# Moving a chunk's reciprocal and its product with it from the end of one beat into the middle of the next

## The chip, the cores and the metric

The kernel runs on one core of one Trainium2 chip. The metric is the device time of one execution in microseconds (us). Before the change it is 4211.53 us, the median of three runs (4208.49 to 4213.91 us). All lines of a profile in this document come from one profiled execution, whose own time is told below.

The core has five engines that run side by side and wait for each other through semaphores. In the profile PE is the matrix engine and PEld its weight loads, DVE is the vector engine, ACT the engine of pointwise functions, POOL the general engine, and SP the queue from which this kernel issues all of its DMAs. Each of them works through its own list of instructions in order.

## The reference

Two layers over 8 batches of 2048 nodes with 256 features. Layer 0 is an attention whose softmax runs over *chunks* of 256 keys, each by itself; the results of the 8 chunks are added. Layer 1 is a graph attention over the whole row. Each layer is followed by a residual and a layer norm.

```python
# layer 0 (4 heads of 64), per batch
scores = jnp.einsum('bhnd,bhjcd->bhnjc', q, kc) / jnp.sqrt(Dh)
scores = jnp.clip(scores, -10.0, 10.0)
scores = jnp.where(mask == 0, -10.0, scores)
attn = jax.nn.softmax(scores, axis=-1)              # over c, the 256 keys of chunk j
ctx = jnp.einsum('bhnjc,bhjcd->bhnd', attn, vc)     # summed over the 8 chunks
out = layernorm(ctx.reshape(B, N, 256) @ Wo.T + bo + x) * gamma + beta
x = layernorm(x + out)
# layer 1
Wh = x @ W
e = leaky_relu(s_i[:, :, None] + s_j[:, None, :], 0.2)   # s = Wh @ a1, Wh @ a2
e = where(adj > 0 or diagonal, e, -inf)
x = layernorm(x + elu(softmax(e) @ Wh))
```

## The kernel before

**Tiles and beats.** The queries of a batch are cut into 4 blocks of 512. A block takes the 8 chunks of keys in turn, so there are 8 x 4 x 8 = 256 chunks, and a chunk takes two *beats*: an even one (`half` 0) and an odd one (`half` 1). A beat treats one tile of 128 keys for all four heads, as two score tiles of 128 x 1024. While chunk J gets its scores, the chunk before it (`prev`) gets its products with the values. Layer 1 of the batch before runs beside layer 0 in the same beats; batch 0 has no layer 1 beside it, and after the 512 beats of layer 0 the last batch's layer 1 runs alone.

**What a beat does, in the order in which it is written down.** Each engine gets its instructions in this order (the schedule is written by hand).

1. `begin_beat`: the exponentials of layer 1's weights that were made ready a beat ago (ACT, L765), then `leaky` of the next layer 1 steps (DVE, L754), one or two a beat: `RATE` is 1.5 steps a beat, and none where layer 1 has nothing ready.
2. The score matmuls of this beat (PE, L873), their *clips* against the mask (DVE, L884: it reads a tile in PSUM and a mask in SBUF), and the exponentials (ACT, L888). Where layer 1 has no steps open (`spare`), one score tile more is done ahead, with a third PSUM buffer.
3. `middle_of_beat`: `edges`, the second DVE operation of each layer 1 step (L760).
4. The products of `prev` (PE, L942). In the even beat these are part 2, the softmax denominators (with `ones` as weights), and part 0; in the odd beat part 1. ACT copies parts 0 and 1 to `un` (L950) and the denominators to `ds` (L956), and SP issues a DMA that lays them out as 128 x 16, `dc<-ds` (L958).
5. `end_beat`: layer 1's products (PE, L776); then the *generators*: `ahead` (`prelude` of the next layer 1 batch, with its `half_max` on DVE, L451, and its loads) and `fins` (`fin`, `fin1`, projections: output projections, statistics, norms); then the *agenda* of this beat.

**The reciprocal's path.** Three functions stand on the agenda. `inverse` is the DVE reciprocal of `dc` (L964) and a DMA of it to DRAM, `rd<-dc` (L966). `spread` is the DMA that broadcasts it to 128 partitions, `r<-rd` (L970, 256 KB); SP issues it when `rd` has landed. `scaled` is the DVE product `un<-un,r` (L977; L975 for a block's first chunk) and POOL's addition `ctxT<-ctxT,un` (L978). Outside batch 0 (`early` false) `inverse` and `spread` are at the end of the even beat E in which the denominators were made, and `scaled` is at the end of E+2. In batch 0 they are at the end of E+1 and of E+4. So DVE meets, at the end of each even beat, first the product of the chunk before and then the reciprocal of this chunk, and next `leaky` and the clips of the odd beat. The chunk's `un`, `dc`, `ds` and `r` have two buffers each.

**What waits for ctxT.** After a block's last chunk `scaled` notes its beat in `ctx_done`; `fin` does its output projection (PE, L370) in the next beat.

**Loads.** Masks of layer 0 are loaded at the start of an odd beat (one chunk in four), those of layer 1 in `begin_beat`, both by L140; `xT_q`, the input of the next block's query projection (`make_qT`, PE at L266), at the end of an odd beat, one chunk before it is used.

Of the kernel before, what the change touches and what calls it, by code (L numbers as in the profile page):

```python
# [28 lines left out]
def tile_adj_attention__then__gat(  # L29
# [88 lines left out]
    def xT_tile(b, ib, name):  # L118
        t = four.tile([P, KC, IB], F32, tag="xT", name=f"xT_{name}{b}_{ib}")
        nc.sync.dma_start(out=t, in_=xT[b, :, ts(ib, IB)].rearrange("(k p) n -> p k n", p=P))  # L120
        return t
# [16 lines left out]
    def mask_block(n, ib, hf, name):  # L138
        t = two.tile([P, HT, IB], I8, tag=f"mask{n}", name=f"mk{n}_{name}")
        nc.sync.dma_start(out=t, in_=mask[n][ib, hf])  # L140
        return t
# [209 lines left out]
    ctx_done = {}  # L351
# [370 lines left out]
    total = B * NIB * NCH  # L722
# [72 lines left out]
    l1_live = True  # L795
    ahead = [prelude(b) for b in range(B - 1)] + [last_prelude(B - 1)]
    edged, weighted = [], []
    agenda = {}
    beat = 0
    credit = 0.0  # L800
    RATE, LAST_RATE = 1.5, 1.3
# [1 line left out]
    def l1_open():  # L803
        return edged or weighted

    def at(when, fn):
        agenda.setdefault(when, []).append(fn)

    def begin_beat(rate):
        nonlocal l1_live, credit, edged, weighted, leaking  # L810
        weighted, edged = edged, []
        for s in weighted:
            s.weights()
        leaking = []
        credit = min(credit + rate, 2.0)
        while l1_live and credit >= 1.0:
            s = next(l1, False)
            if s is False:
                l1_live = False
            elif s is None:  # L820
                break
            else:
                credit -= 1.0
                leaking.append(s)
                s.leaky()

    def middle_of_beat():
        nonlocal edged
        for s in leaking:
            s.edges()  # L830
        edged = leaking
# [30 lines left out]
    prev = None  # L862
# [19 lines left out]
    def clip(sc, b, ib, n):  # L882
        cap = blocks0[b, ib, n // HT][:, n % HT, :].unsqueeze(1).to_broadcast([P, 2, IB])
        nc.vector.scalar_tensor_tensor(sc, sc, -CLIP, cap, ALU.max, ALU.min)  # L884

    def exponentials(chunk, n, hp, sc):
        e = eight.tile([P, 2, IB], F32, tag="e", name=f"e{b}_{ib}_{n}_{hp}")
        nc.scalar.activation(e, sc, AF.Exp)  # L888
        chunk["es"].append(e)

    for J in range(total + 1):
        b, ib, j = J // (NIB * NCH), J // NCH % NIB, J % NCH
        live = J < total
        if live and j == 0:
            ctxT = one.tile([P, 2, IB], F32, tag="ctx", name=f"ctxT{b}_{ib}")
        cur = {"b": b, "ib": ib, "j": j, "es": [], "ctxT": ctxT, "v": vs[min(b, B - 1)], "name": f"{b}_{ib}_{j}"}
        for half in range(2):
            c = 2 * j + half
            if live:

                if c % HT == 1:
                    n = (b * NIB + ib) * 2 + c // HT + 1
                    nb, nib, nhf = n // (2 * NIB), n // 2 % NIB, n % 2
                    if 0 < nb < B:
                        blocks0[nb, nib, nhf] = mask_block(0, nib, nhf, f"{nb}_{nib}_{nhf}")
            if ahead_sc is not None:
                exponentials(cur, c, 0, ahead_sc)
            begin_beat(RATE if b < B - 1 else LAST_RATE)
            if live:


                spare = not (l1_open() or leaking)
                todo = [(b, ib, c, hp) for hp in range(0 if ahead_sc is None else 1, NPAIR)]
                if spare and (b, ib, c + 1) != (0, 0, HT):
                    if c + 1 < NT:
                        todo.append((b, ib, c + 1, 0))
                    elif b == 0:
                        todo.append((*nxt, 0, 0))
                scs = [scores(*which) for which in todo]
                for which, sc in zip(todo, scs):  # L920
                    clip(sc, *which[:3])
                ahead_sc = None
                for which, sc in zip(todo, scs):
                    if which[2] == c:
                        exponentials(cur, c, which[3], sc)
                    else:
                        ahead_sc = sc
            middle_of_beat()

            early = J < NIB * NCH  # L930
            if prev is not None:
                if half == 0:

                    pool, tag = (one, "hr") if early and J % 3 == 2 else (two, "un")
                    prev["un"] = pool.tile([P, 2, IB], F32, tag=tag, name=f"un{prev['name']}")
                for part in ((2, 0), (1,))[half]:
                    m = ps_m.tile([P, IB], F32, tag="m", name=f"u{prev['name']}_{part}")
                    for i in range(2):
                        pc = 2 * prev["j"] + i
                        for h in range(H):  # L940
                            f0 = h * D + part * DH
                            nc.tensor.matmul(  # L942
                                m[h * DH : (h + 1) * DH, :],
                                prev["v"][pc // TPB][:, pc % TPB, f0 : f0 + DH] if part < 2 else ones[:, 0:DH],
                                prev["es"][2 * i + h // 2][:, h % 2, :],
                                start=(i == 0),
                                stop=(i == 1),
                            )
                    if part < 2:
                        nc.scalar.copy(prev["un"][:, part, :], m)  # L950
                    else:

                        ds = two.tile([P, IB], F32, tag="ds", name=f"ds{prev['name']}")
                        nc.scalar.copy(ds, m)  # L956
                        dc = two.tile([P, IB // DH], F32, tag="dc", name=f"dc{prev['name']}")
                        nc.sync.dma_start(  # L958
                            out=dc, in_=ds.rearrange("(h m) (n w) -> h m n w", m=DH, n=DH)[:, 0, :, :]
                        )  # L960
                        prev["dc"] = dc

                        def inverse(p=prev):
                            nc.vector.reciprocal(p["dc"], p["dc"])  # L964
                            p["rd"] = dram3.tile([H, IB], F32, tag="rd", name=f"rd{p['name']}")
                            nc.sync.dma_start(out=p["rd"].rearrange("h (m w) -> (h m) w", m=DH), in_=p["dc"])  # L966

                        def spread(p=prev):
                            p["r"] = two.tile([P, IB], F32, tag="r", name=f"r{p['name']}")
                            nc.sync.dma_start(out=p["r"], in_=p["rd"].unsqueeze(1).to_broadcast([H, DH, IB]))  # L970

                        def scaled(p=prev):
                            r2 = p["r"].unsqueeze(1).to_broadcast([P, 2, IB])
                            if p["j"] == 0:
                                nc.vector.tensor_mul(p["ctxT"], p["un"], r2)  # L975
                            else:
                                nc.vector.tensor_mul(p["un"], p["un"], r2)  # L977
                                nc.gpsimd.tensor_add(p["ctxT"], p["ctxT"], p["un"])  # L978
                            if p["j"] == NCH - 1:
                                ctx_done[p["b"], p["ib"]] = beat  # L980
                            if p["j"] == NCH - (5 if p["b"] == 0 else 4):
                                fins.append(fin(p["b"], p["ib"], p["ctxT"]))

                        lag = 1 if early else 0
                        at(beat + lag, inverse)
                        at(beat + lag, spread)
                        at(beat + 2 + 2 * lag, scaled)

            end_beat()
            if half == 1:  # L990

                sooner = 1 if b == 0 else 0
                if live and j == NCH - 2 - sooner and (b, ib) != (B - 1, NIB - 1):
                    nxt = (b, ib + 1) if ib + 1 < NIB else (b + 1, 0)
                    xq = xT_tile(*nxt, "q")
                if live and j == NCH - 1 - sooner and (b, ib) != (B - 1, NIB - 1):
                    make_qT(*nxt, xq)
            beat += 1
        prev = cur if live else None
# [51 lines left out]
```

## Time and profile before

| | |
|---|---|
| median of three runs | 4211.53 us |
| the profiled execution's own time | 4214.11 us |
| its span, first to last instruction | 4212.3 us |
| PE busy | 3930.2 us (93%) |
| DVE busy | 3234.6 us (77%) |
| ACT busy | 2183.5 us (52%) |
| POOL busy | 1112.8 us (26%) |
| mean granted TensorE clock | 0.981 |

The profiled execution is 2.6 us longer than the median of the runs. The span holds seven stretches of about 512 us, one for each batch of layer 0 (batch 0 up to about 510 us, then one batch with the layer 1 of the batch before beside it), an eighth that ends near 3985 us, and a tail of layer 1 alone. In the page of a profile, a row of a group gives how many instructions it had, its busy time, the mean length of one in ns, and after the bar the idle time of the engine just before them and what ended it. In a row of the timeline the first two numbers are start and length in us, and a bracket holds the idle time of the engine before it and who ended it.

### The profile page before, as it was taken

How to read it: one execution, taken by the hardware profiler on the slowest of the kernel's cores; microseconds unless marked ns; L12 is line 12 of the kernel's file. 1: busy time of each engine (PE TensorE's matmuls, PEld its weight loads, DVE VectorE, ACT ScalarE, POOL GpSimd, SP SyncE). 2: the span in 40 equal slices, each digit the busy share in tenths (PEclk: the TensorE clock that was granted, in tenths of full speed). 3: DMA queues.
4: the chain of work that ended last, by engine and by line, in shares of the span. 5: the costliest groups of instructions: out<-in, count | busy, mean ns of one | idle time of the engine just before them, and what ended most of it. 6: DMA issues, size and time to landing. Idle time of an engine off the chain costs nothing.

```text
span 4212.3 us, 67836 instructions
## 1 busy us (share of the span) xinstructions
PE 3930.2 (93%) x26677; PEld 1349.5 (32%) x26677; DVE 3234.6 (77%) x5038; ACT 2183.5 (52%) x3153; POOL 1112.8 (26%) x481
## 2 busy tenths in 40 slices
PE   9899899998999989999899998999989999899867
PEld 3223233332233322333233332323323333233222
DVE  5886698756987579875789757887588875887886
ACT  5665455555555545554555554455545555455434
POOL 0232322223223222222323222232222222232300
PEclk9999999999999999999999999999999999999989
DMA  5554332223322243221432214322142322432321
GB/s 175 183 169 149 102 108 86 67 67 108 104 82 67 61 126 101 77 64 52 132 98 81 67 51 133 91 81 68 57 134 84 90 65 66 124 94 72 123 87 56
DMA packets 282192, 400.00 MB, mean 95 GB/s; under 512 B 101872, under 2 KB 152944, under 8 KB 280975
## 3 DMA queue, kind: packets, MB, share of 16 engines
q1 hardware_dynamic: 281870, 395.66, 30.7%
q8 instruction: 209, 3.42, 0.3%
q14 instruction: 113, 0.92, 0.1%
HBM read 340.79 MB, written 52.69 MB: 93 GB/s over the span
## 4 chain that ended last, share of the span: by engine, by line
PE 63%; DVE 18%; DMA 7%; ACT 5%; issue 4%; POOL 1%; SPq 1%; DVEq 0%; ACTq 0%; POOLq 0%
PE u L942 20%; PE sc L873 15%; PE us L776 15%; DVE sc L884 6%; PE pk L266 3%; PE pv L285 3%; PE pq L266 3%; PE po L370 3%; DVE w L754 3%; PE pw L605 3%; DMA dc<-ds 2%; DVE w L760 2%; DVE fb L451 2%; DMA rd<-dc 2%; ACT e L888 1%
## 5 line engine op out<-in xcount | busy, mean ns | idle before, releaser
L888 ACT ACTIVATE e<-sc 128x1024 f32<-128x1024 f32 x1024 | 1040.2, 1023 | 1225.7 <-DVE sc L884 1196.3
L884 DVE SCALAR_TENSOR_TENSOR sc<-sc,mk 128x1024 f32<-128x1024 f32 x1024 | 1206.6, 1223 | 568.1 <-PE sc L873 487.2
L873 PE MATMUL sc<-qT,kT 64*128 64x512 f32 x4096 | 1045.5, 625 | 100.1 <-ACT e L888 99.9
L776 PE MATMUL us<-w,hb 128*32 128x512 f32 x8192 | 955.8, 601 | 76.5 <-ACT w L765 68.3
L978 POOL TENSOR_TENSOR ctxT<-ctxT,un 128x1024 f32<-128x1024 f32 x224 | 556.7, 2485 | 1715.8 <-DVE un L977 1552.5
L942 PE MATMUL u<-e,v 128*32 128x512 f32 x8192 | 979.1, 595 | 0.0
L873 PEld LDWEIGHTS sc<-qT,kT 64*128 64x128 f32 x4096 | 348.8, 187 | 727.0 <-issue 354.3
L754 DVE SCALAR_TENSOR_TENSOR w<-ab,sj 128x512 f32<-128x512 f32 x512 | 502.7, 1001 | 8.8 <-DMA ab<-ab_d 5.4
L942 PE MATMUL u<-e,ones 128*32 128x512 f32 x4096 | 505.3, 612 | 0.0
L776 PEld LDWEIGHTS us<-w,hb 128*32 128x32 f32 x8192 | 262.8, 111 | 712.0 <-issue 545.9
L942 PEld LDWEIGHTS u<-e,v 128*32 128x32 f32 x8192 | 240.3, 110 | 658.0 <-issue 520.8
L760 DVE SCALAR_TENSOR_TENSOR w<-w,sj,mk 128x512 f32<-128x512 f32 x512 | 393.4, 790 | 3.4 <-DMA mk<-mask 0.9
L950 ACT COPY un<-u 128x512 f32<-128x512 f32 x512 | 300.1, 586 | 152.5 <-PE u L942 143.9
L765 ACT ACTIVATE w<-w 128x512 f32<-128x512 f32 x512 | 306.4, 628 | 69.6 <-DVE w L760 60.7
L451 DVE CUSTOM_DVE_ANT_0 fb<-sj_row,fb 128x1024 bf16<-128x1024 f32 x240 | 336.4, 1412 | 5.0 <-DMA fb<-far 4.9
L977 DVE TENSOR_TENSOR un<-un,r 128x1024 f32<-128x1024 f32 x224 | 278.5, 1244 | 54.0 <-DMA r<-rd 53.8
L942 PEld LDWEIGHTS u<-e,ones 128*32 128x32 f32 x4096 | 108.5, 111 | 363.2 <-issue 301.5
L626 POOL TENSOR_TENSOR hx<-hx,hr 128x1024 f32<-128x1024 f32 x28 | 88.5, 3160 | 370.1 <-DVE hx L625 370.1
L964 DVE RECIPROCAL dc<-dc 128x16 f32<-128x16 f32 x256 | 63.6, 248 | 143.8 <-DMA dc<-ds 137.0
L956 ACT COPY ds<-u 128x512 f32<-128x512 f32 x256 | 148.7, 581 | 29.7 <-PE u L942 21.7
L266 PE MATMUL pq<-xT_q,WT_q 128*128 128x512 f32 x248 | 122.2, 634 | 39.6 <-DMA xT_q<-in_xT_dram 24.1
L266 PE MATMUL pk<-xT_k,WT_k 128*128 128x512 f32 x256 | 122.3, 621 | 18.0 <-ACT ds L956 10.2
(108 smaller groups left out, 2434.7 us busy)
## 6 DMA issues: line engine op xcount, KB each, us to landing
r<-rd SPq DMA_DIRECT2D x256, 256.0 KB
mk<-mask SPq DMA_DIRECT2D x120, 512.0 KB
fb<-far SPq DMA_DIRECT2D x240, 256.0 KB
xT_k<-in_xT_dram SPq DMA_DIRECT2D x32, 512.0 KB
raw<-in_adjT_dram SPq DMA_DIRECT2D x32, 512.0 KB
rawf<-in_adj_dram SPq DMA_DIRECT2D x32, 512.0 KB
x<-in_x_dram SPq DMA_DIRECT2D x32, 512.0 KB
h_d<-y SPq DMA_DIRECT2D x32, 512.0 KB
```

What stands on the lines that cost most here:

```text
L266: nc.tensor.matmul(pm, WT[name][:, k, ts(o, P)], xt[:, k, :], start=(k == 0), stop=(k == KC - 1))
L451: nc.vector.tensor_tensor_reduce(out=fb, in0=row, in1=fb, scale=1.0, scalar=2 * FAR * 0.999, op0=ALU.add, op1=ALU.max, accum_out=dst,)
L754: nc.vector.scalar_tensor_tensor(self.w, k["ab"][:, 0, :], k["sj"][:, 1, c : c + 1], k["ab"][:, 1, :], ALU.max, ALU.add)
L760: nc.vector.scalar_tensor_tensor(self.w, self.w, k["sj"][:, 0, c : c + 1], k["mks"][c // HT][:, c % HT, :], ALU.add, ALU.min)
L765: nc.scalar.activation(self.w, self.w, AF.Exp)
L776: nc.tensor.matmul(k["us"][g * DH : (g + 1) * DH, n, :], k["hb"][c // TPB][:, c % TPB, f0 : f0 + DH], self.w, start=first, stop=last,)
L873: nc.tensor.matmul(sc[:, h, :], kTs[b][n // TPB][h * D : (h + 1) * D, hp, ts(n % TPB, P)], qTs[b, ib][h * D : (h + 1) * D, hp, :], start=True,
L884: nc.vector.scalar_tensor_tensor(sc, sc, -CLIP, cap, ALU.max, ALU.min)
L888: nc.scalar.activation(e, sc, AF.Exp)
L942: nc.tensor.matmul(m[h * DH : (h + 1) * DH, :], prev["v"][pc // TPB][:, pc % TPB, f0 : f0 + DH] if part < 2 else ones[:, 0:DH], prev["es"] ...
L950: nc.scalar.copy(prev["un"][:, part, :], m)
L978: nc.gpsimd.tensor_add(p["ctxT"], p["ctxT"], p["un"])
```

## The change

`inverse` and `spread` of a chunk outside batch 0 leave the agenda of the even beat E. They go to a new list, `behind_clips`, and are written down in beat E+1 at the start of `middle_of_beat`: behind the clips and ahead of `edges`. `scaled` of every chunk leaves the agenda of its beat (its `due`) and goes to another new list, `behind_leaky`, of beat `due`+1: behind that beat's `leaky` and ahead of its clips. Only the last two chunks, whose `due` lies behind the last beat of layer 0, keep the agenda for `scaled`. `ctx_done` now holds `due` and not the beat in which `scaled` is written, so `fin` comes in the same beat as before.

On DVE an odd beat changes from [product, reciprocal at the end of the even beat], leaky, clips, edges to leaky, product, clips, reciprocal, edges. In batch 0, which has no leaky, the product keeps its place before the clips, and the reciprocal its own. On PE, ACT and POOL the order of the instructions is the same in both kernels. On SP `rd<-dc` and `r<-rd` move behind the mask loads of beat E+1, and stay ahead of the loads that the generators issue at its end.

```diff
-    agenda = {}
+    agenda, behind_leaky, behind_clips = {}, {}, {}
...
                 s.leaky()
+        for fn in behind_leaky.pop(beat, []):
+            fn()

     def middle_of_beat():
         nonlocal edged
+        for fn in behind_clips.pop(beat, []):
+            fn()
         for s in leaking:
             s.edges()
...
                             if p["j"] == NCH - 1:
-                                ctx_done[p["b"], p["ib"]] = beat
+                                ctx_done[p["b"], p["ib"]] = p["due"]
...
                         lag = 1 if early else 0
-                        at(beat + lag, inverse)
-                        at(beat + lag, spread)
-                        at(beat + 2 + 2 * lag, scaled)
+                        if early:
+                            at(beat + lag, inverse)
+                            at(beat + lag, spread)
+                        else:
+                            behind_clips[beat + 1] = [inverse, spread]
+                        prev["due"] = beat + 2 + 2 * lag
+                        if prev["due"] < 2 * total:
+                            behind_leaky.setdefault(prev["due"] + 1, []).append(scaled)
+                        else:
+                            at(prev["due"], scaled)
```

## The prediction

> **What bounds the kernel now.** I read the page first, then PE's own waits stage by stage, then the timeline around each of PE's gaps.
>
> ```profile
> span 4212.3 us, 67836 instructions
> PE 3930.2 (93%) x26677; PEld 1349.5 (32%) x26677; DVE 3234.6 (77%) x5038; ACT 2183.5 (52%) x3153; POOL 1112.8 (26%) x481
> L754 DVE SCALAR_TENSOR_TENSOR w<-ab,sj 128x512 f32<-128x512 f32 x512 | 502.7, 1001 | 8.8 <-DMA ab<-ab_d 5.4
> L977 DVE TENSOR_TENSOR un<-un,r 128x1024 f32<-128x1024 f32 x224 | 278.5, 1244 | 54.0 <-DMA r<-rd 53.8
> L964 DVE RECIPROCAL dc<-dc 128x16 f32<-128x16 f32 x256 | 63.6, 248 | 143.8 <-DMA dc<-ds 137.0
> ```
>
> The last row is what the change goes for: DVE stands 137 us before the reciprocal, waiting for `dc`. But DVE is not the bound. PE is busy 93% of the span, and only its 282 us of idle time can be won or added to. PE's waits in one batch's stretch (1536 to 2048 us):
>
> ```profile
> PE sc L873 <- ACT e L888: 13.6, 7, 6.1
> PE us L776 <- ACT w L765: 4.1, 3, 2.6
> PE pq L266 <- ACT un L950: 2.5, 2, 1.5
> PE po L370 <- POOL ctxT L978: 1.1, 1, 1.1
> PE us L776 <- ACT agg L791: 1.1, 1, 1.1
> PE pq L266 <- DMA xT_q<-in_xT_dram: 1.0, 1, 1.0
> PE pk L266 <- ACT ds L956: 1.0, 1, 1.0
> ```
>
> That is 24.4 us of 512, and the same list comes back in each of batches 1 to 6. So the question is which of these few gaps hang on an odd beat's clips. Only one of over a microsecond does in the open part of a batch (layer 1 beside), this one:
>
> ```profile
> 1794.47 1.22 DVE L977 TENSOR_TENSOR un<-un,r 128x1024 f32<-128x1024 f32 x1
> 1795.84 2.38 POOL L978 TENSOR_TENSOR ctxT<-ctxT,un 128x1024 f32<-128x1024 f32 x1 [5.39 <-DVE un L977]
> 1795.94 0.25 DVE L964 RECIPROCAL dc<-dc 128x16 f32<-128x16 f32 x1 [0.25 <-DMA dc<-ds]
> 1796.12 2.64 DVE L754 SCALAR_TENSOR_TENSOR w<-ab,sj 128x512 f32<-128x512 f32 x1
> 1798.68 2.35 DVE L884 SCALAR_TENSOR_TENSOR sc<-sc,mk 128x1024 f32<-128x1024 f32 x2
> 1799.93 2.16 ACT L888 ACTIVATE e<-sc 128x1024 f32<-128x1024 f32 x2 [2.22 <-DVE sc L884]
> 1801.98 0.58 ACT L950 COPY un<-u 128x512 f32<-128x512 f32 x1
> 1802.62 3.70 PE L266 MATMUL pq<-xT_q,WT_q 128*128 128x512 f32 x8 [1.53 <-ACT un L950]
> ```
>
> The leaky (L754) takes 2.64 us here and 0.66 us elsewhere (1602.21): it runs beside POOL's addition and ends 0.5 us behind it. Two clips beside such an addition keep their 2.3 us (1534.16 below; POOL adds from 1534.23). The largest gap lies at a batch's boundary, where layer 1 has run dry:
>
> ```profile
> 1526.52 0.54 SPq L970 DMA_DIRECT2D r<-rd  x1
> 1532.86 1.23 DVE L977 TENSOR_TENSOR un<-un,r 128x1024 f32<-128x1024 f32 x1 [6.74 <-DMA r<-rd]
> 1534.00 0.25 DVE L964 RECIPROCAL dc<-dc 128x16 f32<-128x16 f32 x1
> 1534.16 2.33 DVE L884 SCALAR_TENSOR_TENSOR sc<-sc,mk 128x1024 f32<-128x1024 f32 x2
> 1536.48 2.08 PE L873 MATMUL sc<-qT,kT 64*128 64x512 f32 x4 [6.12 <-ACT e L888]
> ```
>
> Here DVE waits for the broadcast itself, behind a burst of the prelude's loads.
>
> **The change, part by part.** No instruction is added or removed; DVE's reciprocal and product change places in the odd beat, and SP's `rd<-dc` and `r<-rd` come about one pair of clips later.
>
> *Reciprocal and product in the open part.* The reciprocal's wait goes (its cover is the leaky, the product and two clips, 4.2 us, where `dc` lands about 2 us after its issue), and POOL's addition then runs beside the clips and not beside the leaky. At 1794.47 the row becomes leaky 0.6, product 1.2, clips from 1796.3 and not 1798.68: 2.4 us earlier. The copy of `un` ends at about 1800.4, before PE ends the work ahead of `pq` at 1801.08, so the 1.53 us go. Batches 1 to 6 each have this gap: 6 x 1.53 = -9.2 us. A smaller gap of the same kind (0.31 us before the scores at 1634.80; leaky 2.62) goes too: -1.8 us. Ends: 0, if ACT is late for another reason, and -12. Everywhere else in the open part PE has no gap, and DVE's savings buy nothing there.
>
> *The last batch.* Three gaps have the same chain: 0.68 (3689.31), 1.21 (3811.89) and 2.38 us (3841.92; there DVE stands 3.23 us before the reciprocal). The clips come 2.4, 2.4 and 3.1 us earlier: -4.3 us. Ends: -1 and -5.
>
> *What does not move.* The gaps at 1582.73, 1714.01 and 1996.75 lie behind an even beat's clips, after statistics; those at 1586.84, 1720.73 and 2002.55 behind four or eight normalizations on ACT. The change touches neither. Batch 0 keeps its order.
>
> *The broadcast, later.* This is the cost. From the reciprocal it takes 0.3 us to issue `rd`, 1.4 to the issue of `r`, and 5.0 to 5.7 until a product that waits for it can start (1492.59 to 1497.57; 1509.84 to 1515.56): 6.7 to 7.4 us. Before, the product came 12 to 20 us after the reciprocal in the open part. There the reciprocal moves back by 3 to 5 us, the product by a leaky's 0.7 to 1.4; `r` still comes in time, by about a microsecond in the tightest chunk (1813.38 to 1825.51). At the boundary chunks are short: three reciprocals have their product 7.9, 7.4 and 7.7 us behind (1498.71, 1508.14, 1560.09). Moved behind the clips they have some 5.5 us, and the product, now in front of the clips, waits. The first two lie ahead of the 6.12 us gap; their slip (1 and 2.4 us) ends in it, because it ends when the prelude's burst lets `r` through, which does not move. That gap changes by the reciprocal's 0.16 us at 1534.00. The third has nothing behind it that absorbs: clips end 1562.74, reciprocal, `rd` 1563.0, `r` 1564.4, product at 1569.4 and not 1567.77; the clips, which waited for the reciprocal till 1569.85, start at 1570.55, and POOL's addition ends at 1573.1, where `po` started at 1572.38: +0.7 us a boundary (0 if `r` needs 4.3; +1.4 with 5.7).
>
> *The loads behind it.* On SP `r` of 1535.70 is now issued at about 1538.05, straight ahead of the loads that end with `xT_q`. PE waits for that load (1.04 us at 1547.97), then for ACT's copy (0.96 at 1550.88), which hangs on clips that DVE held for 3.40 us before a reciprocal. The second gap goes; the first grows by what the burst is late: the first load is issued 1 us later, and up to 1.5 us of `r`'s traffic falls into the burst. Net +0.4, ends -1.0 and +1.5. Together a boundary costs -0.1 + 0.7 + 0.4 = +1.0 us, seven times: +7.0; ends -7 and +20.
>
> [...]
>
> *The tail.* The last reciprocal but one (3963.15) goes behind clips that end at 3966.24; `r` is then there at about 3973, its product 2 us later than at 3970.81. DVE waits for the next reciprocal until 3973.58 today, so it loses little, but POOL's three additions (3972.46 to 3980.9, contended by DVE) shift: +1 us, ends 0 and +2.
>
> Sum: -9.2 - 1.8 - 4.3 + 7.0 + 1.0 = -7.3 us on the profiled execution's 4214.1 us (2.6 above the median): 4206.8 there, 4204.2 against the median of 4211.5, or 0.17% faster. A measurement of this kernel can tell about 0.2% (8.4 us) from no change.
>
> **Rivals.** *The broadcast's delay decides, slower.* In a boundary the product, its clips, the next reciprocal and the broadcast now form a loop: 1.2 + 2.3 + 0.2 + 6.7 = 10.4 us, where the short chunks turn in about 9.3. If the slip is not absorbed by the 6.12 us gap (it is if that gap still ends near 1536.5), a boundary pays 1.1 + 1.3 + 1.1 and 0.4 for the load: 3.9 us, times seven 27; with the gains of 15.3 and the tail, +13 us: 4224. It decides against the change from 2.0 us a boundary, and by 0.2% from 3.2.
> *A free boundary, clearly faster.* `xT_q` is no later and `r` needs 4.3 us: -1.0 a boundary, -22 us in all with the tail at +0.5: 4189. For it: the 0.96 us gap goes whatever the load does. Against it: the DMA engines are filled by that burst.
> *Nothing.* ACT or PE hold the odd-beat gaps, and the boundary pays nothing: 4211. For it: PE is full in the open part. Against it: the chain of 1802.62 is unbroken back to the leaky.
>
> **How the numbers follow.** Forecast 0.47, which lies around the bound (0.20 faster, 0.27 same); free boundary 0.20, faster; nothing 0.09, same; broadcast 0.24, of it 0.22 slower and 0.02 same. Faster 0.40, same 0.38, slower 0.22. The forecast's own range is 4197 to 4211; with the rivals' middle parts 4189 to 4224.
>
> **What the trace after would show.** Right: DVE's idle time before the reciprocal near 20 us, leaky's mean near 800 ns, no PE gap before the `pq` like 1802.62's; DVE's wait for `r` above 54 us, with waits of 1 to 3 us in each boundary; the gap like 1536.48's still 6 us; `pq` waiting 2 to 3 us for `xT_q`. Wrong: that gap at 8 us or more, new PE gaps before scores in the open part (then `r` is late there too), or a mid-batch `pq` that still waits for `un`. The prediction fails most easily on a transfer: all seven boundaries repeat one pattern, so 1 us misjudged there is 7 us.

## The result and the profile after

The changed kernel takes 4229.58 us, the median of five runs (4225.94 to 4235.57), beside 4210.15 for the kernel before on the same chip (five runs, 4204.95 to 4213.91). The ratio is 1.0047, with a 95% interval of 1.0036 to 1.0059: half a percent slower, where the forecast was 0.17% faster. The profiled execution took 4225.94 us, 11.8 more than that of before. The page of the changed kernel; the last three rows are groups by line, with the number of instructions, busy time, mean and the idle time in front:

```profile
span 4224.2 us, 67772 instructions
PE 3941.1 (93%) x26677; PEld 1350.2 (32%) x26677; DVE 3193.3 (76%) x5038; ACT 2183.0 (52%) x3153; POOL 1072.2 (25%) x481
L754 DVE SCALAR_TENSOR_TENSOR w<-ab,sj 128x512 f32<-128x512 f32 x512 | 442.4, 884 | 13.8 <-ACT w L765 8.3
L981 DVE TENSOR_TENSOR un<-un,r 128x1024 f32<-128x1024 f32 x224 | 304.2, 1358 | 103.8 <-DMA r<-rd 101.6
L968 DVE RECIPROCAL dc<-dc 128x16 f32<-128x16 f32 x256 | 62.2, 243 | 42.2 <-DMA dc<-ds 42.0
```

DVE's wait in front of the reciprocal fell from 137 to 42 us and a leaky's mean from 1001 to 884 ns, as the change meant. In return DVE stands 101.6 us before the product, waiting for the broadcast, and not 53.8. And PE is busy 10.9 us longer with the same 26,677 matmuls, while its idle time stayed what it was: 4224.2 - 3941.1 = 283 us, before 282. The waits of the changed kernel (total, times, longest):

```profile
DVE un L981 <- DMA r<-rd: 101.6, 40, 6.8
PE sc L877 <- ACT e L892: 101.1, 48, 6.8
DVE dc L968 <- DMA dc<-ds: 42.0, 18, 3.9
PE pq L266 <- DMA xT_q<-in_xT_dram: 41.8, 10, 6.6
PE po L370 <- POOL ctxT L982: 15.0, 15, 2.1
```

PE's wait for `xT_q` grew from 24.1 to 41.8 us; its wait for the copy of `un` ahead of `pq` (15.4 us, 12 times) is no longer in the list. The gap in mid-batch is gone as the prediction had it: leaky, product and clips follow each other, POOL's addition lies beside the clips, and `pq` starts without a wait (timeline of the changed kernel: start, duration, engine, line, idle time in brackets).

```profile
1802.02 0.75 DVE L754 SCALAR_TENSOR_TENSOR w<-ab,sj 128x512 f32<-128x512 f32 x1
1802.68 1.22 DVE L981 TENSOR_TENSOR un<-un,r 128x1024 f32<-128x1024 f32 x1
1803.81 2.36 DVE L888 SCALAR_TENSOR_TENSOR sc<-sc,mk 128x1024 f32<-128x1024 f32 x2
1804.04 2.37 POOL L982 TENSOR_TENSOR ctxT<-ctxT,un 128x1024 f32<-128x1024 f32 x1 [6.05 <-DVE un L981]
1806.08 0.24 DVE L968 RECIPROCAL dc<-dc 128x16 f32<-128x16 f32 x1
1808.47 3.60 PE L266 MATMUL pq<-xT_q,WT_q 128*128 128x512 f32 x8
```

The boundary between batches 3 and 4, before the change (chunks 131 and 132) and in the changed kernel (chunks 129 to 132):

```profile
2029.22 0.25 DVE L964 RECIPROCAL dc<-dc 128x16 f32<-128x16 f32 x1
2030.94 2.12 SPq L443 DMA_DIRECT2D fb<-far  x4
2039.32 0.54 SPq L970 DMA_DIRECT2D r<-rd  x1
2045.30 1.23 DVE L977 TENSOR_TENSOR un<-un,r 128x1024 f32<-128x1024 f32 x1 [6.78 <-DMA r<-rd]
...
2048.93 2.08 PE L873 MATMUL sc<-qT,kT 64*128 64x512 f32 x4 [6.36 <-ACT e L888]
```

```profile
2015.03 1.23 DVE L981 TENSOR_TENSOR un<-un,r 128x1024 f32<-128x1024 f32 x1 [1.16 <-DMA r<-rd]
2016.17 2.36 DVE L888 SCALAR_TENSOR_TENSOR sc<-sc,mk 128x1024 f32<-128x1024 f32 x2
2018.43 0.24 DVE L968 RECIPROCAL dc<-dc 128x16 f32<-128x16 f32 x1
2018.71 0.32 SPq L970 DMA_DIRECT2D rd<-dc  x1
2021.53 0.54 SPq L974 DMA_DIRECT2D r<-rd  x1
2028.21 1.23 DVE L981 TENSOR_TENSOR un<-un,r 128x1024 f32<-128x1024 f32 x1 [5.38 <-DMA r<-rd]
2029.35 2.36 DVE L888 SCALAR_TENSOR_TENSOR sc<-sc,mk 128x1024 f32<-128x1024 f32 x2
2031.61 0.24 DVE L968 RECIPROCAL dc<-dc 128x16 f32<-128x16 f32 x1
2031.68 2.08 PE L877 MATMUL sc<-qT,kT 64*128 64x512 f32 x4 [3.65 <-ACT e L892]
...
2041.90 1.95 SPq L443 DMA_DIRECT2D fb<-far  x4
2042.89 0.24 DVE L968 RECIPROCAL dc<-dc 128x16 f32<-128x16 f32 x1
2043.95 0.39 SPq L970 DMA_DIRECT2D rd<-dc  x1
...
2050.34 0.54 SPq L974 DMA_DIRECT2D r<-rd  x1
2056.33 1.23 DVE L981 TENSOR_TENSOR un<-un,r 128x1024 f32<-128x1024 f32 x1 [6.84 <-DMA r<-rd]
...
2059.81 2.08 PE L877 MATMUL sc<-qT,kT 64*128 64x512 f32 x4 [6.28 <-ACT e L892]
```

A product waits for its `r`, its clips wait behind it, the next reciprocal waits behind the clips, and the next `r` is late in turn. Before, this boundary had one such gap (6.36 us); now a second one of 3.65 us stands ahead of it, and the large one is as large as it was and ends 10.9 us later (2059.81 for 2048.93, of which 5.8 us were already lost where the boundary began).

**Where the time went, by stretch.** ACT has the same 3153 instructions in the same order in both kernels. So the start of an ACT instruction in one trace less its start in the other tells what was lost up to that point. I take a boundary from 452, 957, 1469, 1981, 2493, 3009 and 3525 us of the trace of before to 600, 1112, 1624, 2136, 2650, 3165 and 3680; the open parts of batches 1 to 6 lie between, the last batch's from 3680 to 3982, the tail behind. Each end is the median over 13 neighbouring instructions. All profiled executions of this study in us, against that of before:

| kernel | batch 0 | 7 boundaries | open parts | last batch | tail | span |
|---|---|---|---|---|---|---|
| the prediction's sum | 0 | +7.0 | -11.0 | -4.3 | +1.0 | -7.3 |
| changed | -1.0 | +32.9 | -15.0 | -4.8 | -0.3 | +11.9 |
| product alone moved | +13.2 | +31.0 | -7.4 | +5.4 | -1.5 | +40.7 |
| reciprocal alone moved | +1.4 | +48.6 | -18.1 | -5.2 | -0.8 | +25.9 |
| changed in the open parts only | -0.1 | -0.6 | -15.1 | -4.5 | +0.7 | -19.6 |
| changed in the dry stretches only | +0.3 | +44.7 | -1.4 | 0.0 | -1.0 | +42.6 |
| changed, `xT_q` early | +0.6 | +30.7 | -15.0 | -4.9 | -0.6 | +10.8 |
| before, `xT_q` early | +1.9 | +3.1 | -0.1 | -0.1 | +0.1 | +4.9 |
| reciprocal ahead of the clips | -0.8 | -7.4 | -13.2 | -2.9 | -0.5 | -24.9 |
| changed, no wait for `r` in five chunks | +3.9 | +8.3 | -16.8 | -4.7 | +0.4 | -9.0 |
| loosened | +1.4 | -5.3 | -18.3 | -5.0 | -1.2 | -28.3 |
| loosened, `xT_q` early | -0.6 | -0.7 | -8.4 | -4.1 | -1.1 | -14.9 |

The gains are where the prediction put them and a little larger. The whole miss is the boundaries. Cut at the same ends, PE's idle time in the changed kernel is 15.0 us shorter in the open parts, 4.1 shorter in the last batch and 19.0 longer in the boundaries, so that its sum hardly moves; and PE's busy time is 14.0 us longer in the boundaries and the same in the open parts. (A single execution of one kernel scatters by 5 us and more, so a difference of 2 us in a row says nothing. The run with the product later in the dry stretch is left out, since ACT's order differs in it at 126 places.)

Each boundary holds one large PE gap, the stall at chunk 4, and ahead of it the first load of the prelude's burst, `fb<-far` (2030.94 us above, 2041.90 in the changed kernel). How much later these are in the changed kernel, in us, counted from what was already lost where the boundary begins:

| boundary near | 512 | 1024 | 1536 | 2048 | 2560 | 3072 | 3584 | sum |
|---|---|---|---|---|---|---|---|---|
| the burst's first load | 4.0 | 0.2 | 0.2 | 5.2 | 5.0 | 2.4 | 1.7 | 18.7 |
| the stall's end | 4.4 | -0.7 | -0.3 | 5.1 | 4.7 | 2.2 | 1.0 | 16.4 |
| the boundary's end | 7.9 | 2.5 | 3.0 | 6.6 | 5.7 | 4.7 | 2.5 | 32.9 |

The stall ends as much later as the burst begins later, to within a microsecond. Half of the loss, 16.4 us, is there at the stall's end; the other half, 16.5 us, comes behind it.

### The profile page after: what moved, and what is told of

It reads as the page before. It is cut to its first block, busy times and chain, and to the rows that moved or that the text cites. A ratio compares the mean times of both kernels' runs of the same rounds, so it can differ in the third digit from the quotient of the medians.

```text
span 4224.2 us, 67772 instructions
## 1 busy us (share of the span) xinstructions
PE 3941.1 (93%) x26677; PEld 1350.2 (32%) x26677; DVE 3193.3 (76%) x5038; ACT 2183.0 (52%) x3153; POOL 1072.2 (25%) x481
## 4 chain that ended last, share of the span: by engine, by line
PE 70%; DVE 13%; DMA 8%; ACT 4%; issue 3%; POOL 1%; SPq 0%; DVEq 0%; POOLq 0%; ACTq 0%
PE u L946 21%; PE us L776 18%; PE sc L877 17%; DVE sc L888 4%; PE pq L266 3%; PE po L370 3%; PE pk L266 3%; PE pw L605 3%; PE pv L285 3%; DMA r<-rd 3%; DMA rd<-dc 2%; DMA xT_q<-in_xT_dram 2%; DVE w L760 1%; ACT y L342 1%; DVE w L754 1%
## 5 line engine op out<-in xcount | busy, mean ns | idle before, releaser
L982 POOL TENSOR_TENSOR ctxT<-ctxT,un 128x1024 f32<-128x1024 f32 x224 | 532.3, 2376 | 1796.9 <-DVE un L981 1778.9
L754 DVE SCALAR_TENSOR_TENSOR w<-ab,sj 128x512 f32<-128x512 f32 x512 | 442.4, 884 | 13.8 <-ACT w L765 8.3
L981 DVE TENSOR_TENSOR un<-un,r 128x1024 f32<-128x1024 f32 x224 | 304.2, 1358 | 103.8 <-DMA r<-rd 101.6
L266 PE MATMUL pq<-xT_q,WT_q 128*128 128x512 f32 x248 | 128.4, 666 | 41.8 <-DMA xT_q<-in_xT_dram 41.8
L960 ACT COPY ds<-u 128x512 f32<-128x512 f32 x256 | 148.7, 581 | 31.5 <-PE u L946 27.4
L370 PE MATMUL po<-WT_o,ctxT 128*128 128x256 f32 x512 | 119.8, 387 | 16.4 <-POOL ctxT L982 15.0
```

The costliest lines, as they stand in the source:

```text
L266: nc.tensor.matmul(pm, WT[name][:, k, ts(o, P)], xt[:, k, :], start=(k == 0), stop=(k == KC - 1))
L754: nc.vector.scalar_tensor_tensor(self.w, k["ab"][:, 0, :], k["sj"][:, 1, c : c + 1], k["ab"][:, 1, :], ALU.max, ALU.add)
```

## The experiments

**Two halves, in the code.** The first two runs make one part of the change each.

```diff
# product alone: the reciprocal's place as before
-                        if early:
-                            at(beat + lag, inverse)
-                            at(beat + lag, spread)
-                        else:
-                            behind_clips[beat + 1] = [inverse, spread]
+                        at(beat + lag, inverse)
+                        at(beat + lag, spread)
# reciprocal alone: the product's place as before
-                        if prev["due"] < 2 * total:
-                            behind_leaky.setdefault(prev["due"] + 1, []).append(scaled)
-                        else:
-                            at(prev["due"], scaled)
+                        at(prev["due"], scaled)
```

> Only the product is moved (to the start of the beat after, behind leaky, ahead of the clips); the reciprocal and its two DMAs stay at the end of the even beat. Theory (the later broadcast is what a boundary pays for): the reciprocal is not later, so a boundary costs between -1 and +1 us and DVE's wait for r stays near 54 us; the open part keeps a part of the gain only, since the reciprocal's wait for dc comes back ahead of leaky (0.6 of the 1.5 us of the pq gap, six times, and half of the last batch's 6): 4206 us, -5 against the kernel before, ends -12 and +5. Rival (a product in front of the clips is what costs, wherever r is): the boundaries keep most of their 28 us, so +10 to +25.

Measured: 4255.02 us, ratio 1.0091 (1.0076 to 1.0106). A miss for my theory, and its rival's reason is not the right one either. DVE's wait for `r` is not in the list of waits any more; it waits for `dc`. The waits of this kernel, and a place at the end of batch 0 where it loses several us:

```profile
DVE dc L968 <- DMA dc<-ds: 366.0, 179, 7.2
```

```profile
435.33 0.25 DVE L968 RECIPROCAL dc<-dc 128x16 f32<-128x16 f32 x1 [4.92 <-DMA dc<-ds]
435.50 1.16 DVE L981 TENSOR_TENSOR un<-un,r 128x1024 f32<-128x1024 f32 x1
439.18 0.59 ACT L954 COPY un<-u 128x512 f32<-128x512 f32 x1 [8.36 <-POOL ctxT L982]
439.82 3.78 PE L266 MATMUL pk<-xT_k,WT_k 128*128 128x512 f32 x4 [6.96 <-ACT un L954]
```

Before, the reciprocal stood behind the product, whose 1.2 us covered a part of the wait for `dc`. With the product alone moved it stands in front of it: the product, POOL's addition and ACT's next copy now wait for a `dc` that they don't need. So the two parts of the change are not independent: the product can only go back if the reciprocal goes back as well. This run does not price the product's place by itself.

> Only the reciprocal, the store rd and the broadcast r are moved (behind the clips of the next beat); the product stays at the end of its even beat. Theory: the boundaries lose what they lose in the changed kernel, 28 us in seven, or a little more, with waits for r at chunks 32b+1 to 32b+3 again; the open part gains little, because leaky runs beside POOL's addition again (mean near 1000 ns): +24 us, 4235, ends +18 and +32. Rival (the product's place costs): within 4 us of the kernel before, or faster.

Measured: 4245.57 us, ratio 1.0064 (1.0052 to 1.0077), +27 us: within the theory's range. DVE's wait for `r` is 114.1 us in 39 waits, at chunks 32b+1 to 32b+3 again. One part of the expectation fell: the open parts gain as much as with both moves (-18.1). The leaky's mean falls here too, to 916 ns: with no reciprocal between, the leaky follows the product at once and starts ahead of POOL's addition. A pair of rows that repeats through the open part (0.74 us, where the prediction's row had 2.64):

```profile
1812.54 0.74 DVE L754 SCALAR_TENSOR_TENSOR w<-ab,sj 128x512 f32<-128x512 f32 x1
1812.76 2.77 POOL L982 TENSOR_TENSOR ctxT<-ctxT,un 128x1024 f32<-128x1024 f32 x1 [5.39 <-DVE un L981]
```

So the product's own move isn't needed for the gain.

**By stretch.** The next two make the change for a part of the chunks.

```diff
+                        beside = l1_open() or leaking
-                        if early:
+                        if early or not beside:      # open parts only ("early or beside" for the opposite)
-                        if prev["due"] < 2 * total:
+                        if beside and prev["due"] < 2 * total:      # ("not beside and" for the opposite)
```

> The change is made only for chunks whose reciprocal is scheduled while layer 1 runs beside (chunks 9 to 30 of a batch); those of the dry stretch around a boundary keep the order of before. Theory (losses and gains lie in different stretches and add): the boundaries are those of the kernel before, the open parts and the last batch keep their -17 us, the tail its +2: -15 us, 4195, ends -18 and -9. Rival (the gain of an open part is only the slip of the boundary ahead of it caught up again): no change, 4207 to 4213.

Measured: 4195.22 us, ratio 0.9943 (0.9927 to 0.9958): 24 us faster than before, more than the theory's 15 and its end of 18. The boundaries cost nothing (-0.6), the open parts keep their gain.

> The opposite: the change is made only for the chunks of the dry stretches (chunk 31 of a batch and chunks 0 to 8 of the next), the open parts keep the order of before. Theory: the boundaries' +28 us stand alone: 4238, ends +20 and +34. Rival (the open part catches the slip up): +8 to +15, close to the changed kernel.

Measured: 4257.63 us, ratio 1.0096 (1.0081 to 1.0111), +40 us, above the theory's 28 and its upper end of 34; the rival's 8 to 15 are out. Gains and losses lie in different stretches, and -24 and +40 add to +16, about the changed kernel's +20. The open parts catch up no more than 1.4 us.

**Is it the load behind `r`?** The offsets jump where a boundary's `pq` waits for `xT_q`: in the boundary at 1024 us the changed kernel is 0.6 us ahead just in front of that load and 4.7 us behind just after. That looked like the prediction's load term, sized too small. Both kernels were given the load one beat earlier.

```diff
             end_beat()
+            if half == 0 and live and b and j == NCH - 2 and (b, ib) != (B - 1, NIB - 1):
+                xq = xT_tile(*((b, ib + 1) if ib + 1 < NIB else (b + 1, 0)), "q")
             if half == 1:
...
-                    xq = xT_tile(*nxt, "q")
+                    if b == 0:
+                        xq = xT_tile(*nxt, "q")
```

> The changed kernel, with one thing beside: from batch 1 on the load xT_q is issued at the end of the first beat of its chunk, so ahead of the store rd and the broadcast r that the change moved, and not behind them at the end of the second. Theory (a boundary pays above all for the load behind r: seven waits of pq for xT_q, 29.0 us in the changed kernel against 13.4 in the kernel before, and the half-clock stretches behind them): these waits go to under 5 us in all and the kernel comes to 4200, ends 4193 and 4210. Rival (the product that waits for r in chunks 1 to 3 of a batch is the loss, and the stall at chunk 4 does not absorb it): it stays within 10 us of the changed kernel, 4220 to 4230.

> The kernel before, with the same earlier issue of xT_q. Theory: its 13.4 us of waits for xT_q at boundaries go, a part comes back as pq waiting for the copy of un: -10 us, 4202, ends -18 and 0. The difference to the changed kernel with the early load then tells what the change costs without the load term: between -8 and +2 us if the load is the loss, +12 to +19 if it is not.

Measured: the changed kernel with the early load 4225.9 us, ratio 1.0035 (1.0023 to 1.0047); the kernel before with it 4218.98, ratio 1.0010 (1.0001 to 1.0020). Both theories of mine missed: no wait for the load is left in any boundary and nearly nothing is won. The first one's rival, 4220 to 4230, held. With the early load in both kernels the change costs 7 us, between the two ranges that I had named. The changed kernel's waits:

```profile
DVE un L981 <- DMA r<-rd: 122.5, 41, 6.7
PE pq L266 <- DMA xT_q<-in_xT_dram: 12.4, 3, 6.3
```

The wait for `xT_q` fell by 29 us, that for `r` rose by 21: the product of chunk 32b+7 waits 2.8 to 3.6 us where it waited 1.2 to 1.7. Behind the stall the boundaries still lose 12.5 us of the 16.5. So for the most part the load was only where the lateness came to light; the jump in the offsets had been no proof of its cause.

**The clips ahead of the reciprocal.** One word is changed in substance: the reciprocal, `rd` and `r` come in the same beat, behind the product, but in front of the clips.

```diff
-                            behind_clips[beat + 1] = [inverse, spread]
+                            behind_leaky.setdefault(beat + 1, []).extend([inverse, spread])
```

> The changed kernel with the reciprocal, rd and r in the same beat as the change has them, but ahead of the clips, straight behind the product. Theory (the two clips that the reciprocal stands behind, 2.3 us, are what makes r and the loads behind it late): the boundaries fall back to those of the kernel before, since in the dry stretch product, reciprocal and clips then follow each other as they did; the open part keeps its gain but for DVE's wait for dc at the head of the odd beat: 4195, ends 4188 and 4206. Rival (it is the product's place, or the order of the loads, that costs): 4215 to 4230.

Measured: 4191.1 us, ratio 0.9954 (0.9940 to 0.9968): 19 us faster than before, where the changed kernel is 20 slower. The product is where the change put it, in front of the clips; only the 2.3 us of clips between product and reciprocal are gone. Its waits for `r` are those of before (53.8):

```profile
DVE dc L968 <- DMA dc<-ds: 114.7, 110, 5.1
DVE un L981 <- DMA r<-rd: 51.6, 15, 7.4
PE pq L266 <- DMA xT_q<-in_xT_dram: 24.0, 10, 5.9
```

The chunks' pace shows the loop. Medians over the seven boundaries, chunks 32b+1 to 32b+4, worked out from the starts of products (L977, L981) and reciprocals (L964, L968):

| kernel | from a product to the next reciprocal | from a reciprocal to its product, at the least | chunk 1 to 2, chunk 2 to 3 | chunk 0 to 10 of a batch |
|---|---|---|---|---|
| before | 1.1 to 1.6 us | 7.6 us | 8.9, 9.1 us | 130.4 us |
| changed | 3.4 us | 6.6 us | 11.7, 10.0 us | 136.6 us |
| reciprocal ahead of the clips | 1.1 to 2.3 us | 7.4 us | 8.5, 9.5 us | 130.9 us |

A turn can be longer than the sum of its shortest rows: in the boundary shown above, 9.8 us pass from a reciprocal to its product (2018.43 to 2028.21).

**The wait for `r` taken away.** In five chunks of a boundary the product reads a constant tile.

```diff
+    held_r = const.tile([P, IB], F32, name="held_r")
+    nc.vector.memset(held_r, 1.0)
...
-                            r2 = p["r"].unsqueeze(1).to_broadcast([P, 2, IB])
+                            rt = held_r if p["b"] and p["ib"] == 0 and p["j"] in (1, 2, 3, 5, 7) else p["r"]
+                            r2 = rt.unsqueeze(1).to_broadcast([P, 2, IB])
```

> The changed kernel, but the products of chunks 1, 2, 3, 5 and 7 of batches 1 to 7 read a constant tile of ones in place of r (these chunks' sums are not divided by their denominators); every instruction and load stays, the wait for r alone goes in them. Chunk 4 keeps its wait. Theory (the loop through r is the loss): the 28 us of the boundaries go almost wholly: 4203, ends 4195 and 4212. Rival (not r but the loads or DVE's order behind the clips is late): 4220 to 4230, as the changed kernel.

Measured: 4207.35 us, ratio 0.9985 (0.9977 to 0.9994), 26 us below the changed kernel's ratio. The reciprocals are still behind the clips, the loads still behind the broadcasts (`pq` waits 41.9 us for `xT_q`, as in the changed kernel); only the waits for `r` have gone, and the boundaries fall from +32.9 to +8.3. Counted as in the table of the seven boundaries, the part up to the stall's end falls from +16.4 to -8.1 (the burst's first load from +18.7 to -5.0), and the part behind it stays at +16.4. That shows the wait for `r` to be the loss ahead of the stall. Behind it, the waits for `r` in chunks 5 and 7 are not the loss by themselves, and neither is `xT_q` (12.5 us were left with the early load); both were not taken away at once. With the reciprocal ahead of the clips that part is about -4, so the clips' place causes it as well, but by which wait stays open.

**Can the boundary's own stall be bought?** Two versions go after the gap at chunk 4, which both kernels have. The first is the open-part-only kernel, with the product of a batch's dry chunks one beat later.

```diff
+                        late = b > 0 and prev["b"] == b and not beside
-                        prev["due"] = beat + 2 + 2 * lag
+                        prev["due"] = beat + 2 + 2 * lag + late
```

> The change for the open parts only, as in the run before that did that; and in the dry stretch, in chunks 0 to 8 of batches 1 to 7, the product one beat later still, at the end of the odd beat behind its clips. Theory (the largest gap of a boundary, 5.5 to 7.2 us at chunk 4, is DVE held by a product whose r is behind the prelude's loads, and a half-clock stretch of 6.83 us follows it): DVE's wait for r falls from 59 to under 15 us, the seven gaps and their half clocks go, about 9 us a boundary: -60 against the open-part-only kernel, 4140, ends 4125 and 4175. Rival (the loads reach PE by another way, by xT_q or hb, or the copies wait for a buffer of un): 4185 to 4215.

Measured: 4225.09 us, ratio 1.0021 (1.0011 to 1.0032). A miss by 85 us, and above the rival's 4185 to 4215 too. DVE's wait for `r` is gone (4.0 us), but the reciprocal takes its place, waiting for `dc` behind the same burst of loads, and PE's gap in the boundary near 512 is only 0.4 us shorter than the 5.51 of before (all seven together 35.9 us for 44.2); and further on `po` waits 31.5 us in seven places for ACT's copy `ds`, which it did not before:

```profile
506.04 0.25 DVE L968 RECIPROCAL dc<-dc 128x16 f32<-128x16 f32 x1 [6.72 <-DMA dc<-ds]
508.52 1.23 PE L877 MATMUL sc<-qT,kT 64*128 64x512 f32 x2 [5.11 <-ACT e L892]
```

The second opens the loop at both places, for chunks 1 to 5 of a batch; all others have the reciprocal ahead of the clips.

```diff
+                        deep = b > 0 and prev["b"] == b and ib == 0 and 1 <= prev["j"] <= 5
                         if early:
                             at(beat + lag, inverse)
                             at(beat + lag, spread)
+                        elif deep:
+                            behind_clips[beat + 1] = [inverse, spread]
                         else:
-                            behind_clips[beat + 1] = [inverse, spread]
-                        prev["due"] = beat + 2 + 2 * lag
-                        if prev["due"] < 2 * total:
+                            behind_leaky.setdefault(beat + 1, []).extend([inverse, spread])
+                        prev["due"] = beat + 2 + 2 * lag + deep
+                        if prev["due"] < 2 * total and not deep:
```

> As the run with the reciprocal ahead of the clips, but for chunks 1 to 5 of batches 1 to 7 the loop product, clips, reciprocal, broadcast is opened: the reciprocal stands behind the clips of the next beat and the product one beat later than the change has it, at the end of the odd beat. Theory (the loop sets the pace of the dry stretch, and the stall at chunk 4 is one turn of it behind the prelude's loads): neither r nor dc is waited for there, DVE's wait for r falls from 52 to under 15 us without the 5 to 8 us waits for dc that the later product alone met; the gaps of 5 to 7 us shrink to 1 to 2: 4155, ends 4130 and 4185. Rival (the prelude's loads hold the boundary by other waits, xT_q, fb or hb): 4185 to 4200.

Measured: 4185.12 us, ratio 0.9937 (0.9924 to 0.9949), the lowest ratio of the study, though its interval overlaps that of the open-part-only kernel; but 30 us short of the theory, on the rival's edge. No product waits for `r` (0.8 us in all), PE's wait for clips fell to half, and `pq` waits for `xT_q` instead. That load was then issued earlier here too, with the diff shown above.

> The loosened version (chunks 1 to 5 of a batch with the reciprocal behind the clips and the product a beat later, all other chunks with the reciprocal ahead of the clips), and xT_q issued one beat earlier as in the two runs on it. There the pq matmuls of the boundaries waited 30.0 us for xT_q in seven gaps of 3.0 to 5.1 us, and no product waited for r. Theory (with the loop open nothing but that load is late, so this time an earlier load buys what it waited for, unlike beside the closed loop): -25 us and a part of the half-clock stretches against the loosened version: 4158, ends 4145 and 4172. Rival (it is again only the place where the prelude's loads come to light, and the copies of un or the store of the next chunk take over): 4176 to 4190.

Measured: 4198.2 us, ratio 0.9965 (0.9953 to 0.9977): slower than without, and above the rival's 4176 to 4190 too. The first fence is of the loosened kernel, the second of the one with the early load:

```profile
PE sc L877 <- ACT e L892: 53.2, 40, 2.8
PE pq L266 <- DMA xT_q<-in_xT_dram: 42.5, 10, 6.0
```

```profile
PE sc L877 <- ACT e L892: 51.4, 39, 2.8
PE pq L266 <- ACT un L954: 31.7, 7, 5.4
```

The seven waits stay and change their name, to ACT's copy of `un`. In the one at 1032.29 us the copy hangs on clips behind a reciprocal that waited 5.67 us for `dc`, issued among the prelude's loads. That speaks for the burst of loads holding the boundary by whatever stands at its end; it is not shown, since what would shorten the burst itself was not tried. Beyond that the early load costs some 10 us in the open parts, where it had been in time.

## Why the prediction was wrong, point by point

*The gap ahead of `pq` and the smaller one, -11.0.* Right: the open parts gained 15.0 us, and the open-part-only kernel confirms 15.1. The reason given, a leaky that no longer runs beside POOL's addition, agrees with the runs: those that gain here have a leaky's mean of 883 to 916 ns, the one that changes the dry stretches only has 1008 and gains 1.4; and the reciprocal's wait for `dc` need not go for it (114.7 us are left with the reciprocal ahead of the clips, -13.2). That the reciprocal's move alone is enough I had not seen.

*The last batch, -4.3; the tail, +1.0.* Right within the scatter: -4.8 and -0.3.

*The broadcast in the open part, in time by a microsecond.* Right: no product waits over 0.8 us for `r` between chunk 10 and the end of an open part. (In front of the tail the last chunk but one waits 2.5 us, where the prediction had 2.)

*The boundaries, +7.0.* This is the step that failed: +32.9. The slips at chunks 1 and 2 were seen and sized (1 and 2.4 us; the spacings grew by 2.8 and 0.9), and one behind the stall was seen. What failed is the sentence that the slip of the first two "ends in it, because it ends when the prelude's burst lets `r` through, which does not move". The stall does end when the burst lets `r` through, but the burst moved: by 1.7 to 5.2 us in five of the seven boundaries, and the stall's end with it, 16.4 us in all. In the two where the burst stayed (1024 and 1536) the sentence held, and they are among the three cheapest. The burst is part of the same order: the DVE work that feeds it stands behind products and clips (L400 comes at 2031.77 us for 2022.81, behind the product that waited 5.38 us). And the `r` that is stuck in the burst belongs to a reciprocal which is itself a turn of the loop: in the boundary at 2048 its reciprocal came 13.7 us later (2042.89 for 2029.22, 5.8 of them older), its `rd` and `r` with it, and the stall's end moved by as much as the loop was late. At other boundaries (512, 1024) the stall did shorten, to 3.57 and 4.54 us. In all the seven stalls fell from 44.2 to 37.7 us, and five gaps of 1.9 to 3.7 us appeared ahead of them (12.9 us). Behind the stall the sum had 1.1 us a boundary, 7.7 in all; measured are 16.5, of which no run separates the parts.

*The loads behind it, +0.4 a boundary.* The seven waits for `xT_q` went from 13.4 to 29.0 us, less 6.2 of the second gaps that went: +1.3 a boundary, near the upper end of 1.5. For the most part it was no cost of its own: with the load early the boundaries still pay 30.7.

*The rival that came true.* "The broadcast's delay decides" had product, clips, reciprocal and broadcast as a loop of 10.4 us against a period of 9.3; measured are spacings of 11.7 and 10.0 us against 8.9 and 9.1. Its 27 us for seven boundaries stand beside 33 in the traces, its 4224 beside 4229.6. The profile held what was needed to choose it: 1.2 + 2.3 + 0.2 + 6.7 us is a sum of rows, and a loop longer than a chunk loses the difference in each turn until something slower sets the pace. I asked whether one gap absorbs the slip of two chunks, and not whether the gap's end slips with them.

*The sum in gaps.* The prediction counted waits of PE alone. In the boundaries these grew by 19.0 us; the other 14.0 us of the loss there are longer busy time of the same matmuls, for which the sum had no term. The last section shows how.

*What the trace after was to show.* Right: no `pq` gap, waits for `r` far above 54 us, 1 to 3 us of them in each boundary (up to 5.4 besides the stall). Off: the reciprocal's wait (42, not 20), leaky's mean (884, not 800 ns), `pq` waiting 3.4 to 4.6 us for `xT_q`, not 2 to 3. The mark named for "wrong", the stall at 8 us or more, did not appear: a loop that is late shows in more gaps, not in a larger one.

## What to carry to other kernels

Before an instruction is moved behind a wait, draw the loop that it closes: add up one turn from rows (here product 1.2, clips 2.3, reciprocal 0.2, store and broadcast 6.7 us) and hold it against the shortest chunk of the stretch, for a turn that is longer is paid again and again, and a stall absorbs the slip only if what ends the stall does not slip too. Make the change where the chunks are long and leave it out where they are short (24 us faster, where the change everywhere was 20 slower), or cut the one link that made the turn too long. And do not take the last wait in front of the loss for its cause: an earlier load moved that wait to the next instruction in line, twice.

## What the runs showed of the hardware

Behind short gaps of PE the granted clock of TensorE was often one half. In the changed kernel it was 0.50 in a window at the gap of 3.65 us that ends at 2031.68 us, and 1.00 in the window after it (window, its length, busy time and instructions of PE, PEld, DVE, ACT, POOL, granted clock, DMA share, GB/s):

```profile
2031.00:2037.50 6.50, 5.82 (x24) 1.49 (x28) 4.89 (x13) 3.12 (x5) 0.95 (x1) 0.50 0.12 41
2037.60:2044.40 6.80, 6.80 (x47) 2.12 (x41) 3.75 (x5) 4.22 (x7) 2.37 (x1) 1.00 0.31 110
```

PE did 24 matmuls in 5.82 busy us at the granted clock of 0.50 and 47 in 6.80 us at 1.00. In the clock records of the two traces most stretches at 0.50 were 3.41 or 6.83 us long (27 of 29 in the kernel before, 32 of 36 in the changed one). In the seven boundaries they covered 71.7 us before and 99.0 us after the change. Four of the five new gaps ahead of the stalls and six of the seven longer waits for `xT_q` were followed by such a stretch; of the seven waits for `xT_q` before, one was. That goes with the 14.0 us by which PE's busy time grew there: at the granted 0.50 of these windows a stretch cost, an estimate, up to half its length. The five runs of the changed kernel have a granted clock of 0.976 to 0.979, the profiled execution of before 0.981, the five runs of the loosened kernel 0.976 to 0.980.

Not every short gap had one behind it: of PE's 18 gaps of 1.9 to 2.9 us between 400 and 3900 us of the kernel before, 11 were followed by a half-clock stretch, and all seven of 5.5 to 7.2 us by one of 6.83 us. The same gap of 2.6 us had a stretch behind it in some batches (695, 2747 and 3262 us) and none in others (1208, 1720 and 2232). By the same estimate the gap of 2.38 us at 3841.92 us, with a stretch of 3.41 us behind it, cost up to 1.7 us more than itself. I had not reckoned with that, in the boundaries or in the gains.
